# Layer 3 of a four-layer graph network: groups 2 to 4 copied from PSUM as they are, one root for them, weighting one step behind counting, and a loop ordered by an account

## The chip, the cores and the metric

The kernel runs on one NeuronCore of one Trainium2 chip. The core has a matrix engine (PE), a vector engine (DVE), a scalar engine (ACT), a general engine (POOL) and a queue engine (SP) that starts most of the transfers. Each engine takes its instructions in the order in which they were written, and waits at an instruction until what it needs is there. The metric is device time in microseconds (us), the median of several runs of the whole kernel.

## The reference, cut to what matters

A node matrix `x` of 3327 x 64 floats goes through four layers over one adjacency matrix `adj` of 3327 x 3327 floats. Each layer ends in `x = layernorm(x + layer(x))`. Layers 0 and 1 work on distances, layer 2 is two rounds of `tanh([adj @ x, x] @ W)`. The change lies in layer 3 and in the way into it:

```python
x = _layernorm(x + _L2_gnn_ref(x, adj, L2_gnn_W), axis=-1)
# layer 3
support = x @ weight
mask = (adj != 0)
rank = cumsum(mask, axis=1)          # neighbours counted along a row
deg = rank[:, -1:]
k = minimum(deg, 100)
pos = rank - (deg - k)
w = mask * where(pos > 0, 0.5 ** (k - pos), 0.0)
x = _layernorm(x + w @ support + bias, axis=-1)
```

So a neighbour's weight is one half to the power of the number of neighbours that come after it in the row. For every entry of the mask the kernel must know how many neighbours follow.

## The kernel before, in words

**Tiling.** The 3327 nodes are padded to 26 blocks of 128. The adjacency lies transposed in memory, so a block `jb` is 128 source nodes (on the partitions) by 3328 target nodes. Targets are cut into two halves of 1664, and a half into four chunks of 416. Layer 3 runs over 52 steps `q`: 26 blocks for half 0, then 26 for half 1 (`steps`, a list of `(h, jb)`). The passage between the halves is called the turn.

**One step of layer 3.** A step needs the mask of its half block: 1.0 where the adjacency is not zero, as bf16 (`masks`, L366, on DVE). Nine of the 26 blocks have their masks left over from layer 2 (`resident`); the other 17 are loaded again, half by half, as `ah` (L345, on SP's queue, four load buffers, `LOADS`), which makes 34 loads and 34 masks in the layer. Row 0 of a mask is overwritten by a small transfer from `t_rows` (L368), which holds how many neighbours the later blocks have; it is on SP's queue also, and behind it, in the same call, the next load is issued. `count` (L650) multiplies the mask by a constant triangle `tri` on PE: the result in PSUM is, entry by entry, the exponent bits of the weight. `read` brings it to SBUF as int16, whose bits are read as bf16 weights `w` (L669 on ACT, a Relu; or L667 on DVE, a max with 0). A step has two halves `c` of two chunks `e`, so it has four counts and four reads. The counts have one pair of PSUM banks for each `c`: `count(c, q+1)` can only begin when both reads of `(c, q)` are done. `products` then multiplies the weights by the support rows. Those are kept as a sum of three bf16 parts: `s12` holds the first two side by side (the high product, L875, two a half step), `s3` the third (the low product, L892, 64 columns wide). Low products are saved up for `GROUP` steps and then run together.

**The order of the work.** All engines' orders in this part are written out by hand, and a step of the loop (L1051) writes reads, a mask if a buffer is free (`MASKS` buffers), one or two left-over pieces, and then on PE `products(q - LEAD, c)` and `advance(c, q)`, which is `count(c, q + 1)`, for `c` 0 and 1. `LEAD` is 3: products are three steps behind the reads. Whether the second read of a half step goes to DVE or ACT is decided by a small running load of each engine (`loads`).

**The way in.** The tanh of layer 2 comes out in four chunks (`chunk_end`, L629), and `with_x2` (L729) adds the residual. `finish` (L736) multiplies 13 column pairs by `both_m`, which gives centred hidden values and support rows before their norm; this is done in four groups A, B, C, E of 3, 3, 3 and 4 pairs, into two PSUM buffers of two banks each. For each group, `squares` (L745) and `sums` (L748) give the variance, `roots` (L753 to L771) one over its root in nine small DVE instructions, `factor` (L776) the support rows in `rr`, and `x3_of` or `hid_out` and `x3_later` (L776, L791) the layer's input `x3`. `first_part`, `rest_of` and `other_parts` (L794, L798, L802, L803) cut `rr` into its three parts. C and E have one root together. The PSUM of the two `finish` buffers is used again by the accumulators `acc` of the products.

**Row 0.** Row 0 of every block is treated apart: `first_masks` loads these rows, `first_weights` (L477 to L481) makes their weights in `tb`, `first_rows` (L906, L909) gathers their support rows by 16 transfers on POOL's queue, and `first_products` (L916) adds them when four steps of a half are left.

**The end of a half.** `sums_out` (L928 on ACT, L929 on DVE) adds the bias, `by_node` (L935) turns and centres the result, and the norm and the stores follow: `half_out` for half 0 in between the steps of half 1, `last_out` at the very end.

Of the kernel before, what the change touches and what calls it, by code (L numbers as in the profile page):

```python
# [40 lines left out]
LATE = 3  # L41
UNDER_WAY = 4
MORE = 1
CLAMP = 127.0
FIRST_T = 8
BATCH_T = 2
MASKS = 6
LOADS = 4

LN_EPS = 1e-5  # L50
# [18 lines left out]
CUBIC_PLUS = 2 * CUBIC_ROOT - 1  # L69
CUBIC_REST = 1.75705840270866  # L70
NEIGH = 100
GROUP = 7
LEAD = 3
AHEAD = 5
STEP = float(2**7)

# [5 lines left out]
def kernel(  # L82
# [230 lines left out]
    def layers(ctx, x2, x3, begun_here, kept, ready, ahead_ctx, strm):  # L313
# [160 lines left out]
            return m0  # L474

        def first_weights(m0):
            nc.vector.tensor_scalar(m0, m0, 0.0, (NEIGH + 1) * STEP, ALU.not_equal, ALU.mult)  # L477
            yield
            nc.vector.scalar_tensor_tensor(m0, tb, -STEP, m0, op0=ALU.mult, op1=ALU.add)
            yield  # L480
            nc.vector.tensor_scalar(tb.bitcast(I16), m0, 0.0, None, ALU.max)  # L481
            yield

        with tc.tile_pool(
# [200 lines left out]
        rest = [jb for jb in range(NB) if jb not in resident]  # L685
        rest.sort(key=lambda jb: next(i for i, g in enumerate((10, 7, 4, 0)) if jb % NBH >= g))
        for h in range(2):
            n = len(here) - (5 if h == 0 else 0)
            mixed = here[:-n]
            late_here = here[-n:]  # L690
            for i, jb in enumerate(rest):
                mixed.append(jb)
                while late_here and (i + 1) * n >= (n - len(late_here) + 1) * len(rest):
                    mixed.append(late_here.pop(0))
            steps += [(h, jb) for jb in mixed]
        for q, (h, jb) in enumerate(steps):
# [23 lines left out]
        def slots(i):  # L720
            g, n = parts[i]
            return slice(2 * g, 2 * (g + n))
# [21 lines left out]
        def squares(i):  # L744
            nc.scalar.activation(halves(sq[:, slots(i)]), both[i][0], AF.Square, scale=0.125)  # L745

        def sums(i):
            nc.vector.tensor_reduce(var[:, slots(i)], sq[:, slots(i)], axis=AX.X, op=ALU.add)  # L748

        def roots(sl):  # L750

            v = var[:, sl]
            nc.vector.tensor_scalar(v, v, LN_EPS, None, ALU.add)  # L753
            for _ in roots_of(v, sl):
                pass

        def roots_of(v, sl):

# [14 lines left out]
        def scaled(i, src, dst):  # L773
            n = parts[i][1]
            r = halves(y_all[:, slots(i)].unsqueeze(2).to_broadcast([P, 2 * n, D]))
            nc.vector.scalar_tensor_tensor(  # L776
                halves(dst[:, slots(i)]), src, ROOT_FACTOR, r, op0=ALU.mult, op1=ALU.mult
            )

        def factor(i):  # L780

            scaled(i, both[i][1], rr)

        def x3_of(i):
            scaled(i, both[i][0], x3)

        def x3_later(i):
            scaled(i, halves(x3[:, slots(i)]), x3)

        def hid_out(i):  # L790
            nc.scalar.copy(halves(x3[:, slots(i)]), both[i][0])  # L791

        def first_part(i):
            nc.scalar.copy(s12[:, slots(i), 0, :], rr[:, slots(i)])  # L794

        def rest_of(i):
            sl = slots(i)
            nc.vector.tensor_tensor(rr[:, sl], rr[:, sl], s12[:, sl, 0, :], ALU.subtract)  # L798

        def other_parts(i):  # L800
            sl = slots(i)
            nc.scalar.copy(s12[:, sl, 1, :], rr[:, sl])  # L802
            nc.gpsimd.tensor_tensor(s3[:, sl], rr[:, sl], s12[:, sl, 1, :], ALU.subtract)  # L803

        with tc.tile_pool(name="l3t", bufs=2, space=PSUM, reuse_waits="tile") as l3t:
            chunk_end(3)
            with_x2(3)
            chunk_end(2)
            with_x2(2)
            masks(to_mask.pop(0))  # L810
            finish(l3t, A)
            squares(A)
            chunk_end(1)
            sums(A)
            roots(slots(A))
            factor(A)
            with_x2(1)
            finish(l3t, B)
            squares(B)
            x3_of(A)  # L820
            sums(B)
            first_part(A)
            count(0, 0)
            read(0, 0, (False, False))
            rest_of(A)
            chunk_end(0)
            roots(slots(B))
            with_x2(0)
            other_parts(A)
            finish(l3t, C)  # L830
            count(1, 0)
            squares(C)
            factor(B)
            x3_of(B)
            read(1, 0, (False, False))
            sums(C)
            first_part(B)
            finish(l3t, E)
            rest_of(B)
            hid_out(C)  # L840
            squares(E)
            advance(0, 0)
            masks(to_mask.pop(0))
            masks(to_mask.pop(0))
            sums(E)
            read(0, 1, (False, False))
            advance(1, 0)
            roots(slice(0, 2 * sum(parts[C])))
            read(1, 1, (False, False))
            advance(0, 1)  # L850
            read(0, 2, (False, False))
            advance(1, 1)
            read(1, 2, (False, False))
            factor(C)
            factor(E)
            hid_out(E)
            advance(0, 2)

        l3a = ctx.enter_context(
            tc.tile_pool(name="l3a", bufs=2, space=PSUM, reuse_waits="tile")  # L860
# [5 lines left out]

        def products(q, c):
            h, jb = steps[q]
            first, last = q % NB == 0, q % NB == NB - 1
            if first:  # L870
                acc[h, c] = acc_tile(f"acc3_{h}_{c}")[:, :, :CW]
# [12 lines left out]
            later.append((q, c))  # L884
            if not last:
                high(q, c)
            if last or c and len(later) == 2 * GROUP:
                for ql, cl in later:
                    if last and cl != c:
                        continue  # L890
                    for e in range(2):
                        nc.tensor.matmul(  # L892
                            acc[h, cl][e * D : (e + 1) * D, e, :], s3[:, slot(steps[ql][1]), :],
                            ws[ql, cl, e], start=False, stop=False,
                        )
                later[:] = [ql for ql in later if last and ql[1] > c]
                if last:
                    high(q, c)
# [88 lines left out]
        def last_out(h, accT):  # L987
# [45 lines left out]

        first_out = None
        weighted = first_weights(m0)
        with_step = [
            (lambda: other_parts(B), 0.0, 0.5), (lambda: first_part(C), 0.0, 0.5),
            (lambda: rest_of(C), 0.6, 0.0), (lambda: other_parts(C), 0.0, 0.5),
            (lambda: first_part(E), 0.0, 0.6), (lambda: rest_of(E), 0.7, 0.0),
            (lambda: other_parts(E), 0.0, 0.6),  # L1040
        ]
        at_leisure = [
            (lambda: next(weighted), 0.6, 12), (lambda: next(weighted), 1.05, 14),
            (lambda: next(weighted), 0.6, 16), (lambda: x3_later(C), 0.6, NB),
            (lambda: x3_later(E), 0.7, NB + 1),
        ]
        loads = {True: 0.0, False: 0.0}
        products(0, 0)
        advance(1, 2)
        products(0, 1)  # L1050
        for q in range(LEAD, len(steps) + LEAD + 1):  # L1051
            turn = q == NB + LEAD
            while consumed and consumed[0] <= q:
                consumed.pop(0)
            at_work = len(consumed) - len(to_mask) + (len(at_leisure) > 2)
            one_more = bool(to_mask) and at_work < MASKS
            extra, d, a = with_step.pop(0) if with_step else (None, 0.0, 0.0)
            if NB + LEAD <= q < NB + LEAD + 9:
                d, a = d + 0.6, a + 0.2
            loads[True] = max(0.0, loads[True] - 1.8) + d + 1.04 * one_more  # L1060
            loads[False] = max(0.0, loads[False] - 1.8) + 1.04 + a
            reads = []
            for _ in range(2):
                by = loads[True] + 0.6 <= loads[False] + 0.8
                loads[by] += 0.6 if by else 0.52
                reads.append(by)
            read(0, q, (False, reads[0]))
            if turn:
                first_out = half_out(0, sums_out(0))
            read(1, q, (False, reads[1]))  # L1070
            if extra is not None:
                extra()
            if one_more:
                masks(to_mask.pop(0))
            if not with_step and at_leisure:
                late, d, by = at_leisure[0]
                if loads[True] + d < 2.0 or q >= by:
                    at_leisure.pop(0)
                    late()
                    loads[True] += d  # L1080
                    if len(at_leisure) == 2:
                        first_rows()
            p = q - LEAD if q < NB + LEAD else q - LEAD - 1
            for c in range(2):
                if p and not turn:
                    products(p, c)
                if q < len(steps):
                    advance(c, q)
                if turn:
                    next(first_out)  # L1090
            if first_out is not None and not turn:
                next(first_out, None)
        last_out(1, sums_out(1))


# [991 lines left out]
```

## Time and profile before

| what | us |
|---|---|
| time before, median of 3 runs | 542.13 |
| lowest and highest of them | 540.40, 545.91 |
| the profiled execution's own time | 545.59 |
| its span (first to last instruction of the profile) | 543.9 |
| mean granted PE clock in it | 0.979 |
| first layer 3 instruction on PE (`finish` of group A, L736) | 402.85 |
| first count (L650) | 407.99 |
| first high product (L875) | 419.63 |
| last high product ends | 529.91 |

Times in the profile are counted from the start of its span. A profile group reads: line, engine, operation, output<-input, shape, count, busy time, mean duration of one in ns, idle time of the engine just ahead of it and what ended that. A chain is followed back from the last instruction to what released each. A window table gives the busy time of each engine in a stretch, the count of instructions, the granted PE clock and the transfer engines' share.

### The profile page before, as it was taken

Reading aid. Unit: us, or ns where it says so; the run is one execution under the profiler, and the core shown is the slowest. Engines: PE = TensorE matmul, PEld = TensorE weight load, DVE = VectorE, ACT = ScalarE, POOL = GpSimd, SP = SyncE. Lnnn points to the kernel's source line nnn. Section 1 sums busy time; section 2 is a strip of 40 time slices with the busy share of each in tenths; the row PEclk is TensorE's granted clock in tenths of the full one; section 3 lists DMA queues with packets and bytes.
Section 4 is the critical chain, followed back from the end, with each engine's and each line's share of the span. In section 5 each row is a group of like instructions: output and inputs, shape, how many; then the busy total and the mean of one; then the engine's idle time right before and its main releaser. Section 6 shows DMA issues by size and latency. Waiting matters only on the chain.

```text
span 543.9 us, 7678 instructions
## 1 busy us (share of the span) xinstructions
PE 506.3 (93%) x2865; PEld 210.9 (39%) x2865; DVE 398.8 (73%) x604; ACT 294.2 (54%) x410; POOL 230.5 (42%) x121
## 2 busy tenths in 40 slices
PE   7989999999999999989999999999998898998991
PEld 5622222222222222754433344333343444454551
DVE  6889999999999999899453413456249876577633
ACT  5799999999999998540000010000017766376632
POOL 4499999999999999100000000000360350000000
PEclk9899999999999999999999999999999999799996
DMA  8979777676767718499999207988967899777001
GB/s 286 351 232 295 222 234 230 217 238 203 248 209 234 244 36 331 183 430 420 424 429 425 93 1 282 427 352 330 380 211 254 298 359 339 278 250 225 1 1 38
DMA packets 34139, 139.21 MB, mean 256 GB/s; under 512 B 11199, under 2 KB 12977, under 8 KB 28971
## 3 DMA queue, kind: packets, MB, share of 16 engines
q1 hardware_dynamic: 30571, 137.40, 69.3%
q0 software_dynamic: 1184, 0.63, 0.5%
q10 hardware_dynamic: 2336, 0.59, 0.5%
q8 instruction: 24, 0.39, 0.3%
q14 instruction: 24, 0.20, 0.1%
HBM read 136.93 MB, written 1.04 MB: 254 GB/s over the span
## 4 chain that ended last, share of the span: by engine, by line
PE 60%; DVE 18%; ACT 10%; issue 6%; DMA 4%; DVEq 0%; SPq 0%; ACTq 0%
PE cnt L516 27%; DVE v L1336 10%; PE pq L1315 7%; PE acc L875 5%; PE cnt L650 4%; ACT pq L1328 4%; ACT sg L1288 4%; PE acc L892 4%; PE acc L1345 3%; DMA ah<-in_adjT 3%; PE t L450 2%; DVE a L1327 2%; DVE mask L366 2%; PE cnt L507 1%; DVE w L667 1%
## 5 line engine op out<-in xcount | busy, mean ns | idle before, releaser
L1300 POOL TENSOR_TENSOR sg<-sg,at 128x1664 f32<-128x1664 f32 x44 | 163.7, 3736 | 1.7 <-ACT sg L1288 1.6
L1328 ACT ACTIVATE pq<-pq,al,ga 128x832 f32<-128x832 f32 x104 | 104.7, 1012 | 11.0 <-DVE a L1327 11.0
L1315 PE MATMUL pq<-riT,ljT 64*128 64x416 f32 x416 | 100.8, 561 | 10.3 <-DVE v L1336 6.2
L1336 DVE SCALAR_TENSOR_TENSOR v<-pq,a 128x832 f32<-128x832 f32 x104 | 105.5, 1014 | 3.5 <-ACT pq L1328 2.5
L1327 DVE SCALAR_TENSOR_TENSOR a<-pq,sg 128x832 f32<-128x832 f32 x104 | 105.2, 1012 | 0.5 <-PE prep_fours L1406 0.5
L1345 PE MATMUL acc<-v,xv 128*64 128x416 f32 x416 | 95.3, 537 | 0.0
L516 PE MATMUL cnt<-at_l,lj 128*64 128x416 f32 x496 | 90.5, 515 | 0.0
L669 ACT ACTIVATE w<-cnt 128x416 int16<-128x416 f32 x145 | 66.9, 523 | 38.1 <-PE cnt L650 35.5
L1288 ACT ACTIVATE sg<-lb,rb 128x1664 f32<-128x1664 f32 (+1 forms) x53 | 87.2, 1647 | 0.0
L629 ACT ACTIVATE x<-cnt 128x416 f32<-128x416 f32 x8 | 4.1, 517 | 142.9 <-PE cnt L516 142.9
L462 POOL DMA_DIRECT2D t_rows<-tb x4 | 4.2, 1089 | 150.0 <-DVE tb L460 150.0
L1315 PEld LDWEIGHTS pq<-riT,ljT 64*128 64x128 f32 x416 | 31.3, 184 | 83.7 <-DVE v L1336 82.8
L875 PE MATMUL acc<-w,s 128*128 128x416 bf16 x208 | 53.0, 341 | 1.6 <-DVE sq L776 0.8
L516 PEld LDWEIGHTS cnt<-at_l,lj 128*64 128x64 f32 x496 | 34.4, 137 | 49.8 <-issue 49.4
L667 DVE TENSOR_SCALAR w<-cnt 128x416 int16<-128x416 f32 x63 | 36.4, 585 | 15.4 <-PE cnt L650 14.3
L1345 PEld LDWEIGHTS acc<-v,xv 128*64 128x64 f32 x416 | 20.6, 134 | 61.8 <-issue 58.0
L366 DVE TENSOR_SCALAR mask<-ah 128x1664 bf16<-128x1664 f32 x34 | 35.2, 1040 | 11.7 <-PE cnt L650 6.0
L650 PE MATMUL cnt<-mask,tri 128*128 128x416 bf16 x136 | 36.4, 340 | 6.8 <-DVE w L667 6.5
L516 PE MATMUL cnt<-kept,lj 128*64 128x416 f32 x224 | 41.6, 514 | 0.0
L443 DVE TENSOR_SCALAR tm<-at_l 128x1664 bf16<-128x1664 f32 x16 | 15.7, 1023 | 21.6 <-PE t L450 21.5
L875 PEld LDWEIGHTS <-s 128*128 128x128 bf16 x208 | 19.8, 98 | 29.5 <-issue 14.6
L1300 POOL TENSOR_TENSOR sg<-sg,kept 128x1664 f32<-128x1664 f32 (+1 forms) x10 | 30.0, 3018 | 0.0
(314 smaller groups left out, 457.5 us busy)
## 6 DMA issues: line engine op xcount, KB each, us to landing
at_l<-in_adjT SPq DMA_DIRECT2D x27, 1664.0 KB, 11.8
at<-in_adjT SPq DMA_DIRECT2D x44, 832.0 KB, 6.6
ah<-in_adjT SPq DMA_DIRECT2D x34, 832.0 KB, 7.3
kept<-in_adjT SPq DMA_DIRECT2D x7, 1664.0 KB
bt_l<-in_adjT SPq DMA_DIRECT2D x6, 1664.0 KB
lb<-lf_rows SPq DMA_DIRECT2D x2, 384.0 KB, 6.1
mask<-t_rows SPq DMA_DIRECT2D x34, 3.2 KB
ljT<-ljT SPq DMA_DIRECT2D x4, 128.0 KB, 3.8
```

Source lines behind the costliest of these rows:

```text
L366: nc.vector.tensor_scalar(mask[q], ahead.pop(q), 0.0, None, ALU.not_equal)
L516: nc.tensor.matmul(acc[c][h * D : (h + 1) * D, :], hw[:, slot(jb), :], blocks[jb][:, o : o + CW], start=c not in begun, stop=last, skip_gr ...
L650: nc.tensor.matmul(cnt[c][e], tri, mask[q][:, of], start=True, stop=True, skip_group_check=True,)
L669: nc.scalar.activation(to, of, AF.Relu)
L875: nc.tensor.matmul(acc[h, c][:, e, :], s12[:, slot(jb)].rearrange("p t d -> p (t d)"), ws[q, c, e], start=first, stop=last,)
L1288: nc.scalar.activation(sg[:, :, of], lbs[:, :, of], AF.Sigmoid, bias=rb[:, sl : sl + 1])
L1300: nc.gpsimd.tensor_tensor(sg[:, :, of], sg[:, :, of], at[:, :, of], ALU.mult)
L1315: nc.tensor.matmul(pq[:, h, :], ljT[h != jb // NBH][rows, of], riT[rows, ch * CW : (ch + 1) * CW], start=True, stop=True,)
L1327: stt(a_s[t], pqs[t], CUBIC_PLUS, us.pop(t), op0=ALU.add, op1=ALU.mult)
L1328: nc.scalar.activation(pqs[t], pqs[t], AF.Square, bias=al[:, one], scale=ga[:, one])
L1336: stt(w, pqs.pop(t), CUBIC_REST, a_s.pop(t), op0=ALU.add, op1=ALU.mult)
L1345: nc.tensor.matmul(accs[cp, ci][h * D : (h + 1) * D, :], xv[:, slot(jb), :], w[:, h, :], start=(jb == orders[cp][0]), stop=(jb == orders[c ...
```

## The change

Several edits in layer 3 alone; all work ahead of it is untouched.

1. `finish` of groups B, C and E: both results are copied from PSUM to SBUF as they are by ACT (`parts_out`: x3 and `rr`), two copies each. Squares and sums of B and C together (12 slots), then of E, read the copies; one root covers all 20 slots (`roots(BCE)`), and the factors are applied in SBUF later (`scaled_of`).
2. The cut into three parts: the second part is the DVE subtraction itself, written as bf16; POOL does two subtractions instead of one; the ACT cast is gone.
3. `LEAD` goes from 3 to 1, `GROUP` from 7 to 4, so there are 7 weight buffers instead of 12 of each kind, and `MASKS` goes from 6 to 11.
4. The order of the steps: half 0 begins with the six blocks of group A, the resident ones first.
5. The loop keeps an account of when DVE and ACT will be free (`end`), when a count is there (`counted`), when a load is expected (`landed`), and when PE is free (`at_pe`), and from it chooses at each half step whether DVE first takes a left-over piece, a mask, or the read.
6. After the turn the products of `c` = 1 are one more step behind those of `c` = 0.
7. `CLAMP` is 101 instead of 127, and the weights of row 0 are made in two instructions instead of three.

```diff
-MASKS = 6
+MASKS = 11
-GROUP = 7
-LEAD = 3
+GROUP = 4
+LEAD = 1
...
+        def parts_out(i):
+            nc.scalar.copy(halves(x3[:, slots(i)]), both[i][0])
+            nc.scalar.copy(halves(rr[:, slots(i)]), both[i][1])
...
+        def other_parts(sl):
+            one, two = s12[:, sl, 0, :], s12[:, sl, 1, :]
+            nc.vector.tensor_tensor(two, rr[:, sl], one, ALU.subtract)
+            nc.gpsimd.tensor_tensor(rr[:, sl], rr[:, sl], one, ALU.subtract)
+            nc.gpsimd.tensor_tensor(s3[:, sl], rr[:, sl], two, ALU.subtract)
...
             finish(l3t, B)
-            squares(B)
-            x3_of(A)
-            sums(B)
-            first_part(A)
+            first_part(slots(A))
+            parts_out(B)
             count(0, 0)
-            read(0, 0, (False, False))
-            rest_of(A)
+            read(0, 0, (False, True))
+            other_parts(slots(A))
+            masks(to_mask.pop(0))
             chunk_end(0)
-            roots(slots(B))
             with_x2(0)
-            other_parts(A)
             finish(l3t, C)
             count(1, 0)
-            squares(C)
-            factor(B)
-            x3_of(B)
-            read(1, 0, (False, False))
-            sums(C)
-            first_part(B)
+            masks(to_mask.pop(0))
+            parts_out(C)
+            read(1, 0, (False, True))
+            advance(0, 0)
             finish(l3t, E)
-            rest_of(B)
-            hid_out(C)
-            squares(E)
-            advance(0, 0)
-            masks(to_mask.pop(0))
-            masks(to_mask.pop(0))
-            sums(E)
-            read(0, 1, (False, False))
+            squares_of(BC)
+            parts_out(E)
             advance(1, 0)
...
+        def fill(q, ready):
+            while True:
+                if extras and extras[0][1] == DVE:
+                    cost, by = extras[0][2:]
+                    if max(end[DVE], one_done) + cost <= ready + 0.2 or q >= by:
+                        extra()
+                        continue
+                soon = to_mask and to_mask[0] - q
+                if mask_ready(q) and (
+                    max(end[DVE], landed[0]) + MASK <= ready + 0.5
+                    or soon < 3
+                ):
+                    one_mask()
+                    continue
+                return
...
+            for c in range(2):
+                was_read = reads(c, q) if q < len(steps) else 0.0
...
+                if not turn and p[c] >= (NB if q > NB + LEAD else 0) and p[c] < len(steps):
+                    products(p[c], c)
...
+                if q + 1 < len(steps):
+                    advance(c, q)
```

## The prediction

> **What bounds the kernel now.** I read the page first (busy shares, chain, groups), then the chain of waits and the window table inside layer 3 (402.85 us to the end), then the timeline around each hole. PE is busy 93% of the span, so I asked where in layer 3 it is not. The windows, 3 us each (busy time, number of instructions, PE clock, transfer share, GB/s):
>
> ```profile
> core 0: us, PE busy (x) PEld busy (x) DVE busy (x) ACT busy (x) POOL busy (x), PEclk, DMA share, GB/s
> ...
> 417.00:420.00 3.00, 1.94 (x8) 0.60 (x7) 2.59 (x12) 2.30 (x6) 0.00 (x0) 1.00 0.94 329
> ...
> 429.00:432.00 3.00, 2.05 (x10) 0.87 (x9) 2.21 (x4) 2.87 (x8) 0.04 (x1) 1.00 0.90 307
> ...
> 459.00:462.00 3.00, 1.44 (x8) 0.68 (x7) 0.12 (x1) 1.36 (x4) 0.00 (x0) 1.00 1.00 412
> 462.00:465.00 3.00, 1.54 (x7) 0.50 (x8) 2.50 (x4) 0.00 (x0) 0.00 (x0) 0.61 1.01 409
> 465.00:468.00 3.00, 3.00 (x20) 1.53 (x18) 0.43 (x1) 0.00 (x0) 0.00 (x0) 0.50 0.92 346
> ```
>
> At 459 to 465 every engine is idle and transfers run full; then PE works at half clock. The timeline there shows the hole's two ends:
>
> ```profile
> 461.88 1.03 DVE L366 TENSOR_SCALAR mask<-ah 128x1664 bf16<-128x1664 f32 x1 [3.06 <-DMA ah<-in_adjT]
> 462.82 0.58 DVE L667 TENSOR_SCALAR w<-cnt 128x416 int16<-128x416 f32 x1
> ...
> 463.46 0.51 PE L650 MATMUL cnt<-mask,tri 128*128 128x416 bf16 x1 [3.02 <-DVE w L667]
> ```
>
> A mask stood in DVE's order ahead of a read, and its load had not landed; the read was late by that, and PE's count by the read. The chain has the same figure at 424.21 (a transfer of 6.50 us, then mask, read, count). The way in is a chain of DVE work:
>
> ```profile
> 416.44 0.60 DVE l_var L748
> ...
> 418.74 0.18 DVE root_y L771
> ...
> 419.01 1.16 DVE sq L776 x2
> ```
>
> The first high product (419.63) waits for group C's factor at the end of this root, as the accumulator takes that group's PSUM. From 498 on PE has no hole: the high products of a step follow at 1.41 us and a run of 28 low ones takes 2.58 us. So layer 3 is PE-bound in its last 30 us, and before that held up by DVE.
>
> **What the Trainium skill says.** *TensorE: Matmul & The Clock Gate*, "HAM oscillation — how this bites in real kernels": no PE-idle gaps over about 3.4 us, or the clock is halved and time is lost again. The trace agrees, even a little below that: a 3.02 us hole with thin work around it is followed by 6.8 us at clock 0.50 (462.7 to 469.5), a loss of 3.4 us. *DMA: Bandwidth & Descriptors*, "Queues, rings and completion order": a transfer engine takes descriptors in ring order. The trace agrees: a `t_rows` packet lands 1.0 us after its issue on an empty queue and up to 5 us with loads ahead of it. *VectorE: DVE Perf Modes*, "Why PSUM operands drop a tier": fp32 from PSUM gets one element a cycle, a one-tensor SBUF operation two; here a 416 read takes 0.583 us, a 1664 mask 1.03.
>
> **The change part by part.** Prices from the rows of before: read 0.523 on ACT (0.46 each in a run), 0.585 on DVE; mask 1.04; 384-wide pieces 0.50 to 0.55, 512-wide 0.60 to 0.68; a root nine times 0.2 = 1.8.
>
> *Work.* DVE: before, four sums 2.3, three roots 5.4, factors 2.3, x3 2.3, differences 2.3, weights of row 0 2.2: 16.8 us. After, sums 2.2, two roots 3.6, factors 2.2, x3 2.2, differences 2.2, weights 1.6: 14.0. Saved 2.8. ACT: before 7.6 (squares 2.07, copies 1.09, two casts a group 4.4), after 7.1 (squares 1.9, six copies 3.2, one cast 2.0): even. The wide forms (768, 896) are not in the trace; between the 512 row (0.62, 0.68) and twice 384 (1.0, 1.1) for 768, I take 0.82 on ACT and 0.95 on DVE; 0.1 either way. POOL doubles from 4.1 to some 8.3; the last group's pair (2.2 each, scaled from 0.98 for 384) follows the cast in step 6 or so and is needed by the low products of step 11, five steps later: hidden by about 4 us. If DVE's masks held POOL for the 9 us that one L803 waited, the cover would be gone and some 4 us lost.
>
> *Start.* I walked the new order with these prices. Unchanged to 408.0. ACT: cast A to 408.6, copies B 409.6, first read 410.1, last tanh 411.3; PE ends C at 412.24; copies C 413.2, read, squares of B and C to 414.4; PE ends E near 414.8, copies E to 416.0. PE: counts of step 1 by 415.3, first high product 415.2 to 415.6 (C's PSUM free since 413.2; the second needs E's, 416.0). So it comes 4.3 us sooner, with counts done for two steps instead of three and a half (6 matmuls, 1.1 us). Net some 3 us.
>
> *Floor.* From 415.2 PE has 200 counts and 208 high at 0.176 (71.8), 208 low at 0.0923 (19.2), a change of form around each of some 13 low runs at 0.11 (1.4), first products 1.3, `by_node` at the turn 2.8: 96.5, so 511.7. The same sum for before, from 419.63: 514.5. Its real end is 529.91, so its holes are worth 15.4. They are, by the starts of the high products: steps 0 to 6 2.3, at 431 1.4, 444 1.5, 455 to 460 0.9, 460 to 470 6.1 (3.4 of it clock), turn 2.7, 491 1.6.
>
> *New waits.* DVE's `other_parts(B)` waits for ACT's cast, which stands behind the four reads of step 4 (ACT near 423.3, DVE free at 422.75: 0.6 idle); behind it in DVE's order are the last factor, a mask (step 8's) and the read of step 6, for which PE waits; that is in (a). Copies C and E on ACT stand ahead of the first reads of steps 0 and 1, in the walk above.
>
> *What stays of the holes.* (a) Steps 0 to 8: walking on, reads of steps 4 and 5 are all on ACT (4 x 0.46 to 0.52 = 2.0 against PE's 1.41), with squares and two casts (2.2) between; I get 432.0 where the floor says 429.8: 2.2. (b) Steps 8 to 11 again all on ACT: 1.1. (c) Steps 12 to 25: DVE's order holds 7.3, 6.4 and 7.0 us of work in each four steps, where PE takes 4 x 1.41 + 1.5 = 7.1: full, but not over; 2.0 for queueing. (d) The turn: `c` = 1's products a step later take the 1.1 wait for the norm's sums off PE; 0.7 stays. (e) Half 1: DVE 7.9 and 7.5 in its first eight steps, thinner later; 1.1. Sum 7.1.
>
> *The masks.* Loads: 34 at about 2.2 us when the queue is full; median 7.3 to landing with four under way, about 3.8 on an empty queue. Half 0 needs 12 masks in steps 10 to 24, 3 in four steps of 7.1 us: 2.4 us each, against 2.2. The fifth load lands at 415 and its mask is in DVE's order near 425; load 9 follows that and lands near 430, for step 14 at about 441. Eleven buffers let this lead stand; six did not. So the load holes (at 424 and 460) should go. In SP's order nothing new stands before a load; stores of half 0 are two there as before. Masks put on DVE before a load lands cost DVE up to 0.8 (the account takes 3.55 from mask to landing; the trace has 4.3); in (c).
>
> *The low groups.* Four instead of seven steps cost 6 more changes of form (0.66, in the floor) and spread the relief for reads better. `LEAD` 1 costs nothing: a count already waits for the reads of the step before, so the weights are there. Row 0's chain ends near 450, its products come at about 460; cover 10 us.
>
> *Sum.* 511.7 + 7.1 = 518.8; what follows the last product (543.9 - 529.9 = 14.0) is the same code: span 532.8, and 1.7 outside it: 534.5, to be set against the profiled 545.59. That execution is 3.5 above the median 542.13. If the difference is the half-clock stretch (3.4), which need not fall in each run, the new kernel owes nothing for it: 534.5; if it is spread over the kernel, 531. I take **533.5**.
>
> **The rivals.** *Forecast (0.70):* 528 to 537.
>
> *ACT and DVE take PE's place (0.15).* For it: both have over 7 us in some four-step groups; the account's prices are guesses, and DVE's order is fixed. Against: half 1 of before runs clean with ACT doing 3 of 4 reads. Twice my holes, 14: 541; 537 to 543.
>
> *Late masks in DVE's order (0.07), the slower one.* The new order has three masks in a row in step 12 and pairs in step 16, 20, 24, 32. If loads come later than accounted, each is a 3.0 us hole and 3.4 of half clock, 6.4 in all. Two such beyond my 7.1 give 547.3; it decides from the second on, three give 553.7. Against: masks lead by up to 11 steps' buffers, and before had one such double loss with six.
>
> *It begins sooner, but nothing else (0.03).* Start 2.8, holes as before: 542.8 in the profile's terms, 539 to 542.
>
> *Better (0.05).* Holes 2 or less, and a run like the median: 526.
>
> **Numbers.** A measurement here can tell about 1% from no change, which is 536.7 to 547.5. Faster: nearly all of the forecast, the better case and a little of the second: 0.82. Same 0.10, slower 0.08. Range: holes of 1 with the median's offset, 527, to holes of 13, 540.5.
>
> **What would show it.** First high product near 415 instead of 419.6; no DVE wait for `ah` above 1.5 us, no half clock between 410 and 520; high products at 1.41 us within groups in both halves; 16 low ones in 1.5; ACT full between 416 and 435; last high product at 517 to 521. It is wrong if a DVE mask still waits for its load, or if reads on DVE are the releaser of PE at every group.

## The result, and the profile after

The changed kernel takes 544.28 us (median of 15 runs, 542.81 to 546.08) beside 542.95 for the kernel before on the same chip (15 runs): ratio 1.0025, 95% interval 1.0009 to 1.0041. So it is not faster, and the 1.3 us by which it is slower are below the 1% that the forecast took as the bound. The forecast was 533.5; none of the ranges that the prediction gave to its cases holds the measured time. The profiled execution took 545.25 us with a span of 543.5; the sum in the prediction gave 534.5 and 532.8 for these two, so 10.7 us of span are to be found.

Four times cut the layer, read off the starts of the counts and of the high products in the trace. The forecast's row is the prediction's own walk (408.0, 415.2, floor and holes 103.6, then 14.0). The prediction counted to the end of the last high product, 0.34 us after its start; the other rows are from start to start, so the forecast's two last numbers are put here as 103.3 and 14.3:

| us | first count at | from it to the first high product | steps 0 to 25 | 25 to 27, the turn | 27 to the last | first to last high product | from there to the end |
|---|---|---|---|---|---|---|---|
| before | 407.99 | 11.64 | 57.95 | 8.08 | 43.92 | 109.94 | 14.29 |
| forecast | 408.0 | 7.2 | | | | 103.3 | 14.3 |
| after | 407.67 | 13.12 | 55.61 | 9.45 | 43.86 | 108.93 | 13.81 |

The start is 5.9 us longer than forecast, and the products 5.7 us longer, most of it before step 25 and some at the turn. What came after the turn took as long as it did before the change. Two faults are looked for in what follows: one ahead of the first high product, and one between 430 and 445.

The start first. The window table of the changed kernel (columns: stretch, busy time with count of PE, PE loads, DVE, ACT, POOL, then PE clock, transfer share, GB/s):

```profile
core 0: us, PE busy (x) PEld busy (x) DVE busy (x) ACT busy (x) POOL busy (x), PEclk, DMA share, GB/s
400.00:405.00 5.00, 5.00 (x28) 2.39 (x26) 2.40 (x4) 1.52 (x3) 3.17 (x5) 1.00 0.15 41
405.00:410.00 5.00, 5.00 (x28) 2.31 (x24) 4.23 (x15) 2.28 (x5) 0.72 (x2) 1.00 0.13 37
410.00:415.00 5.00, 2.62 (x14) 1.45 (x10) 0.26 (x2) 2.52 (x5) 1.82 (x2) 0.98 0.70 249
415.00:420.00 5.00, 3.45 (x8) 2.67 (x9) 3.43 (x5) 0.00 (x0) 0.00 (x0) 0.50 1.02 427
...
440.00:445.00 5.00, 3.33 (x10) 1.27 (x11) 4.80 (x7) 1.44 (x3) 5.00 (x9) 0.71 0.82 247
```

From 400 to 410 the transfers are idle (0.15 and 0.13; the kernel before has 0.92 and 1.03 there), from 410 to 415 DVE is idle (0.26 us of 5), and then PE runs at half clock. The timeline of the changed kernel, SP's queue and then DVE, says why DVE was idle:

```profile
395.66 16.09 SPq L345 DMA_DIRECT2D ah<-in_adjT  x4
...
409.59 0.55 DVE L808 TENSOR_TENSOR s<-sq,s 128x384 bf16<-128x384 f32 x1
414.88 1.03 DVE L366 TENSOR_SCALAR mask<-ah 128x1664 bf16<-128x1664 f32 x1 [4.74 <-DMA ah<-in_adjT]
415.82 0.58 DVE L733 TENSOR_TENSOR x<-x,xc 128x416 f32<-128x416 f32 x1
```

DVE's second mask waits 4.74 us for its load, and `with_x2` (here L733) of the last chunk stands behind it. `finish` of group E (here L740) waits for that, and the first high product (here L868) comes after it, as PE's timeline shows:

```profile
416.55 3.75 PE L740 MATMUL both<-both_m,x 128*128 128x256 f32 x8 [3.93 <-DVE x L733]
420.09 0.90 PE L649 MATMUL cnt<-kept,tri 128*128 128x416 bf16 x2
420.79 0.90 PE L868 MATMUL acc<-w,s 128*128 128x416 bf16 x2
```

The four first loads took 16.09 us to be issued. In the kernel before:

```profile
398.77 1.99 SPq L345 DMA_DIRECT2D ah<-in_adjT  x4
```

SP's own waits in the changed kernel, 390 to 420 (who waited for what: us in total, times, longest), name the reason:

```profile
engine line waited for: us in total, times, longest us
SPq L345 <- PE cnt L515: 18.1, 2, 14.5
```

A load waits 14.5 us for a count of layer 2 (`cnt`, L515), with which it shares no data. It shares memory. In the built program the four `ah` buffers lie at bytes 159904 to 186528 of a partition before and at 176544 to 203168 after: five more mask buffers lie below them. In their new place three of them, those of the second, the third and (by 448 bytes) the fourth load, overlap two blocks kept for layer 2 (189408 to 202720 and 202720 to 216032), which its last products read until 410.4. SP issues in order, so the held load holds those behind it.

The second place, 433 to 442, in the timeline of the changed kernel:

```profile
434.06 2.60 POOL L809 TENSOR_TENSOR sq<-sq,s 128x896 f32<-128x896 f32 x1 [1.82 <-DVE s L808]
434.84 2.05 DVE L478 TENSOR_SCALAR tb<-tb 128x832 int16<-128x832 bf16 x1
...
436.74 1.90 POOL L810 TENSOR_TENSOR s<-sq,s 128x896 bf16<-128x896 f32 x1
436.82 2.70 DVE L366 TENSOR_SCALAR mask<-ah 128x1664 bf16<-128x1664 f32 x1
...
441.10 0.34 PE L649 MATMUL cnt<-mask,tri 128*128 128x416 bf16 x1 [2.18 <-DMA mask<-t_rows]
```

The first weighting of row 0 (L478), for which the loop's account has 0.6, took 2.05, and the mask behind it 2.70 where a mask takes 1.03. Both lie beside POOL's two wide subtractions. PE then waits 2.18 us for row 0 of a late mask (the small transfer from `t_rows`), and the mean clock from 440 to 445 is 0.71.

### The profile page after: what moved, and what is told of

It is laid out like the page before. It is cut to its first block, busy times and chain, and to the rows that moved or that the text cites. A ratio compares the mean times of both kernels' runs of the same rounds, so it can differ in the third digit from the quotient of the medians.

```text
span 543.5 us, 7648 instructions
## 1 busy us (share of the span) xinstructions
PE 506.7 (93%) x2865; PEld 210.7 (39%) x2865; DVE 404.9 (74%) x598; ACT 292.2 (54%) x400; POOL 236.0 (43%) x123
## 5 line engine op out<-in xcount | busy, mean ns | idle before, releaser
L515 PE MATMUL cnt<-at_l,lj 128*64 128x416 f32 x496 | 90.5, 515 | 0.0
L668 ACT ACTIVATE w<-cnt 128x416 int16<-128x416 f32 x137 | 64.7, 520 | 32.5 <-PE cnt L649 31.0
L868 PE MATMUL acc<-w,s 128*128 128x416 bf16 x208 | 54.4, 346 | 0.0
L515 PEld LDWEIGHTS cnt<-at_l,lj 128*64 128x64 f32 x496 | 34.4, 137 | 49.8 <-issue 49.4
L666 DVE TENSOR_SCALAR w<-cnt 128x416 int16<-128x416 f32 x71 | 41.2, 588 | 13.3 <-PE cnt L649 10.5
L366 DVE TENSOR_SCALAR mask<-ah 128x1664 bf16<-128x1664 f32 x34 | 36.7, 1092 | 9.5 <-DMA ah<-in_adjT 9.5
L515 PE MATMUL cnt<-kept,lj 128*64 128x416 f32 x224 | 41.6, 515 | 0.0
L649 PEld LDWEIGHTS <-tri 128*128 128x128 bf16 x208 | 19.5, 99 | 24.3 <-issue 7.0
```

The costliest lines, as they stand in the source:

```text
L366: nc.vector.tensor_scalar(mask[q], ahead.pop(q), 0.0, None, ALU.not_equal)
L515: nc.tensor.matmul(acc[c][h * D : (h + 1) * D, :], hw[:, slot(jb), :], blocks[jb][:, o : o + CW], start=c not in begun, stop=last, skip_gr ...
L649: nc.tensor.matmul(cnt[c][e], tri, mask[q][:, of], start=True, stop=True, skip_group_check=True,)
L668: nc.scalar.activation(to, of, AF.Relu)
L868: nc.tensor.matmul(acc[h, c][:, e, :], s12[:, slot(jb)].rearrange("p t d -> p (t d)"), ws[q, c, e], start=first, stop=last,)
```

## The experiments

Each ran beside the kernel before on the same chip. Since that one's median moved by 1.2 us between calls, the ratio is the better measure across them. e9 and e11 have four timed runs each and e14 six, the others 9 to 20; hence the wide intervals of these three.

| run | median us | ratio to before, 95% interval |
|---|---|---|
| the changed kernel | 544.28 | 1.0025, 1.0009 to 1.0041 |
| e1 MASKS = 6 | 540.29 | 0.9963, 0.9945 to 0.9981 |
| e2 C, E on DVE | 545.10 | 1.0048, 1.0029 to 1.0067 |
| e3 e1 and e2 | 540.45 | 0.9976, 0.9959 to 0.9993 |
| e4 before, loads late | 545.38 | 1.0050, 1.0025 to 1.0075 |
| e5 e1, row 0 late | 539.93 | 0.9942, 0.9916 to 0.9968 |
| e6 e1, six load buffers | 541.89 | 0.9995, 0.9969 to 1.0020 |
| e7 e1, square later at the turn | 542.77 | 0.9998, 0.9980 to 1.0017 |
| e8 e1, GROUP = 7 | 549.02 | 1.0104, 1.0073 to 1.0135 |
| e9 e1, C, E on DVE, row 0 late | 535.84 | 0.9861, 0.9800 to 0.9923 |
| e10 e1, six buffers elsewhere | 538.51 | 0.9909, 0.9880 to 0.9939 |
| e11 e9 and e10 | 534.45 | 0.9829, 0.9775 to 0.9883 |
| e12 e9 without row 0 late | 540.77 | 0.9956, 0.9938 to 0.9974 |
| e13 e9 with MASKS = 11 | 541.65 | 0.9972, 0.9945 to 0.9999 |
| e14 e11 again | 535.17 | 0.9854, 0.9821 to 0.9887 |

### The late loads: e1, e4

The written order of the changed kernel never has more than six masks alive, so `MASKS` 6 leaves every engine's order as it is and only moves the buffers.

```diff
-MASKS = 11
+MASKS = 6
```

> The changed kernel with MASKS 6 instead of 11, nothing else. The instruction order is the same on every engine; what moves is where the tiles lie: the four load buffers return to the addresses that they had in the kernel before, off the tiles that layer 2's last products still read. Theory L (late loads: loads 2 to 4 of layer 3 were issued at 410.5 instead of 399 us because of the address): they are issued near 399 again, no hole at 413 to 417, the first high product near 415.2, and the loads stay ahead, so the waits for ah near 451 and 454 go too: 533 to 537 us. Rival D (DVE and its order are the bound, the loads only hide it): the holes move but the time stays within 1% of 544.

540.29, 4.0 us less (3.4 by the ratios). The four loads go out at once again, and from the first count to the first high product it takes 8.40 us, not 13.12. But the time lies above L's 533 to 537, and within 1% of 544 as D had it: the address is one loss, and not the only one. In e1's timeline:

```profile
400.05 2.11 SPq L345 DMA_DIRECT2D ah<-in_adjT  x4
```

The reverse, on the kernel before: the `ah` buffers in a pool of their own, at 179872 to 206496, with every engine's order as it was.

```diff
-                ahead[q] = l3w.tile([P, HALF], F32, tag="ah", ...)
+                ahead[q] = l3h.tile([P, HALF], F32, tag="ah", ...)
...
-                w = l3w.tile(
+                w = (l3v if c else l3w).tile(
```

> The kernel before with its load buffers placed across the same still used tiles as in the changed kernel (the weight buffers of c = 0 lie below them instead), the instruction order unchanged. Theory L: loads 2 to 4 are issued near 410.5, every later load is some 8 us behind, and the time goes up by 4 to 9 us, to 547 to 552. Rival D: the loads have slack, under 2 us.

545.38, 2.9 above its own reference. e4's timeline shows the row of the changed kernel again:

```profile
397.25 16.09 SPq L345 DMA_DIRECT2D ah<-in_adjT  x4
```

The place of the buffers alone makes both the loss and its return. It is less than the 547 to 552 expected: from first count to first high product it took 13.40 us for 11.64, only 1.8 more. In the old way in `with_x2` (412.89 in e4) stands ahead of the late masks; they wait 0.56 and 1.01 us for their loads at 416.40 and 418.44, ahead of the last root.

### POOL beside DVE: e2, e3, e5, e9, e12, e13

The two subtractions of groups C and E go from POOL to DVE, in the changed kernel (e2) and with six masks (e3).

```diff
-            nc.gpsimd.tensor_tensor(rr[:, sl], rr[:, sl], one, ALU.subtract)
-            nc.gpsimd.tensor_tensor(s3[:, sl], rr[:, sl], two, ALU.subtract)
+            eng = nc.vector if sl == CE else nc.gpsimd
+            eng.tensor_tensor(rr[:, sl], rr[:, sl], one, ALU.subtract)
+            eng.tensor_tensor(s3[:, sl], rr[:, sl], two, ALU.subtract)
```

> The changed kernel with the two POOL subtractions of groups C and E (896 wide, other_parts) on DVE instead, the loads still late. Theory P (POOL's wide subtractions hold DVE: a mask took 2.70 and the row 0 weights 2.05 us beside them, instead of 1.03 and 0.6): DVE gets 2.2 us of work and loses 3.1 us of stretching, the PE hole of 438 to 441 and the half clock behind it shrink: 538 to 542. Rival (the 2.05 is the price of that form, and the hole is the mask's late row): no gain, 544 to 547.

> MASKS 6 and the subtractions of C and E on DVE together. Theories L and P together: 530 to 534. L alone right: as e1 or up to 2 us slower.

There is no gain in either: e2's time is its rival's, and e3's is that of L alone. But the durations are settled by it, and against e2's rival: 2.05 us is not the price of that form. The same two DVE instructions, first in e1 with POOL beside them, then in e3 without:

```profile
431.17 2.60 POOL L809 TENSOR_TENSOR sq<-sq,s 128x896 f32<-128x896 f32 x1 [1.82 <-DVE s L808]
431.94 2.06 DVE L478 TENSOR_SCALAR tb<-tb 128x832 int16<-128x832 bf16 x1
433.84 1.90 POOL L810 TENSOR_TENSOR s<-sq,s 128x896 bf16<-128x896 f32 x1
433.92 2.71 DVE L366 TENSOR_SCALAR mask<-ah 128x1664 bf16<-128x1664 f32 x1
```

```profile
431.95 0.37 DVE L478 TENSOR_SCALAR tb<-tb 128x832 int16<-128x832 bf16 x1
432.24 1.02 DVE L366 TENSOR_SCALAR mask<-ah 128x1664 bf16<-128x1664 f32 x1
```

0.37 for 2.06, and 1.02 for 2.71. In e1 the weighting ends at 434.00, 0.23 after POOL's first subtraction, and the mask at 436.63, 0.89 after the second: each is held until POOL is nearly done. The Trainium skill has this on *SBUF — State Buffer*, "Who interferes with whom": DVE in a 2-port mode and GpSimd share a pair of ports, and whichever issues first has it for the whole instruction while "the other fully blocks". The trace agrees: POOL's ends plus the two lengths alone give 434.14 and 436.76, 0.14 and 0.13 from what is seen. So the two subtractions cost DVE 1.69 + 1.69 = 3.4 us here, and spare it two of 1.09 us. (A mask beside the 384-wide pair of group B, 1.74 us at 426.83, loses 0.7 us more, in e3 as in e1.)

That this difference of 1.2 us bought nothing in e3 asks what else stands in that stretch. Row 0's two instructions are not due before step 22, so e5 moves them (and the two scalings of x3 behind them in the list) to step 17 and later.

```diff
-            (lambda: next(weighted), DVE, 0.6, 13), (lambda: next(weighted), DVE, 1.05, 15),
+            (lambda: next(weighted), DVE, 0.6, 18), (lambda: next(weighted), DVE, 1.05, 19),
...
-                if extras and extras[0][1] == DVE:
+                if extras and extras[0][1] == DVE and (q >= 17 or len(extras) not in (3, 4)):
```

> The kernel with MASKS = 6, and the two instructions that weight row 0 (with the two x3 scalings that stand behind them in the list) moved from steps 9 to 13 to steps 17 and later; all work is kept. Theory D: with the loads early again, VectorE sets the counts from 430 to 447: its 0.59-us weighting took 2.06 and the mask behind it 2.71, both beside GpSimd's subtractions, and the counts of steps 10 to 12 wait for the mask behind them. The four steps from 9 to 13 took 12.0 us, of which 5.64 are products and counts and 1.63 a group of low products, so 4.7 are lost there. Moved away, most of that should come back: 536.0 to 538.0 (3 to 4.5 us under the 540.29 of MASKS = 6). Rival Q: the masks only meet the next wait (the load behind each of them, or the row of the mask that is fetched from memory after it): 539 to 540.5.

539.93, a miss for D. e5's timeline shows why:

```profile
431.06 7.20 DVE L366 TENSOR_SCALAR mask<-ah 128x1664 bf16<-128x1664 f32 x4
431.22 2.60 POOL L809 TENSOR_TENSOR sq<-sq,s 128x896 f32<-128x896 f32 x1 [1.82 <-DVE s L808]
...
433.90 2.54 POOL L810 TENSOR_TENSOR s<-sq,s 128x896 bf16<-128x896 f32 x1
...
438.81 0.51 PE L649 MATMUL cnt<-mask,tri 128*128 128x416 bf16 x1 [3.13 <-DVE w L666]
```

Masks moved into the place, four in 7.20 us, where three in a row take 2.89 without POOL (e9, below); one in turn held POOL (2.54 us for 1.90), and a read behind them let PE wait 3.13 us. So e9 does both, and counts the subtractions in the order's account as DVE work:

```diff
-            (lambda: other_parts(CE), DVE, 1.05, 11),
+            (lambda: other_parts(CE), DVE, 3.2, 11),
```

> MASKS = 6, the two subtractions of the group pair C, E on VectorE in place of GpSimd and counted at 3.2 us by the list of the order, and row 0 weighted from step 17 on. No GpSimd subtraction stands beside a mask of this stretch any more. Theory G (GpSimd's subtractions stretch VectorE's masks from 1.02 to 2.71 us and so set the counts of steps 8 to 12): with row 0 moved alone the four masks from 431.1 took 7.20 us instead of 4.1 and a count waited 3.13 us behind them, so that nothing was gained; with both moved, the 3.13-us wait and the half clock behind it (0.85 and 0.81 over ten us, 1.7 us) go, and VectorE's own 2.2 us of subtractions lie between masks with some slack: 535.5 to 537.5, against 539.93 with row 0 alone moved. Rival Q (behind every such wait stands another, the loads and the rows of the masks): 539 to 541, no mask above 1.1 us all the same.

535.84, as G said, though from four runs (534.84 to 538.65). Half clock and the long hole are gone. In e9's timeline three masks in a row take 2.89 us, and in its windows the clock stays at 1.00 though PE idles 1.9 us of five:

```profile
431.34 2.89 DVE L366 TENSOR_SCALAR mask<-ah 128x1664 bf16<-128x1664 f32 x3
```

```profile
435.00:440.00 5.00, 3.14 (x18) 1.39 (x17) 3.84 (x5) 3.18 (x8) 0.56 (x1) 1.00 0.94 344
440.00:445.00 5.00, 5.00 (x37) 2.61 (x36) 4.87 (x7) 3.23 (x8) 3.56 (x5) 1.00 1.00 378
```

e12 keeps the account's new price but leaves row 0 where it was (e9 without its two lines of e5).

> MASKS = 6 and the subtractions of C, E on VectorE, counted at 3.2 us by the list of the order, row 0 weighted as soon as it fits (as in the changed kernel). Tells which part of the 4.1 us between 539.93 and 535.84 (row 0 late alone, and both) is GpSimd's. If the masks of steps 8 to 12 beside GpSimd were the whole loss: 535.5 to 536.5. If row 0's place matters beside it: 537 to 539.

540.77: above both cases. By the medians neither half of e9 is worth anything alone (e5 0.4, e12 none), both are worth 4.4. A part of this is the clock, which falls or stays up behind much the same hole: e5's four runs with a mean granted clock of 0.983 to 0.987 took 537.1 to 538.1 us, its eight at 0.980 and below 539.7 to 540.8. The lowest times (e1 538.39, e5 537.08, e12 538.40, e9 534.84) give 1.3 us to e5, nothing to e12 and 3.55 to both. So both together are worth more than their sum, but e5 alone is not worthless. e9 without the account's new price was not run. In e12 no mask from 427 on takes over 1.03 us, and it keeps pace with e9 to step 10 (high product 29.76 and 29.77 us after the first count). But then row 0 and an x3 scaling (0.37 + 1.02 + 0.95 = 2.3 us) stand ahead of the next mask, and the other scaling (0.68) ahead of the one behind it. They come late, so their buffers are emptied late and the loads for later masks are issued late. (Half clock from 437.1 to 440.6, which e9 does not have, adds at most 1.7 us to e12's loss of 5.9 before step 25.) DVE's waits for loads in e12, 407 to 480, against 1.7 us in e9:

```profile
DVE mask L366 <- DMA ah<-in_adjT: 6.1, 5, 1.7
```

These runs fit one reading, which no single run proves: what runs out is DVE's time up to the last mask whose load is pressing, whatever fills it, POOL's block, row 0, or its own subtractions.

e13 is e9's order on all engines with the buffers of the changed kernel (`MASKS` 11).

> The changed kernel with its eleven mask buffers, so with the loads late at the start, and with C, E on VectorE and row 0 late. If the late loads (4.0 us by MASKS = 6 alone) and VectorE's stretch (4.4 us from 540.29 to 535.84) add: 539 to 540.5. If the late loads hide the second, since VectorE then waits for loads anyway: 542 to 544.

541.65: between the two cases. By the ratios the late loads cost 1.1% in e9 (0.9861 to 0.9972, 6.0 us) and 0.6% in the changed kernel (3.4 us). So the two losses do not hide one another. By the medians the two remedies are worth 4.0 and 2.6 us alone and 8.4 together; that each helps the other is a sign only, since the difference (0.5%) is within the interval of e9's ratio (0.6% either way).

### Load buffers: e6, e10, e11, e14

In e1 the transfer share falls to 0.07 from 425 to 430 and is 0.9 to 1.0 after 440: a load is issued only when a mask has emptied a buffer. e6 gives six buffers.

```diff
-LOADS = 4
+LOADS = 6
...
-            chunk_end(0)
+            chunk_end(0); load(); load()
```

> The kernel with MASKS = 6 and six load buffers in place of four, the two further loads issued behind layer 2's last products. Theory B: in the run with MASKS = 6 the DMA share fell to 0.07 from 425 to 430, since a load is only issued when a mask has emptied a buffer, and was 0.9 to 1.02 from 440 on; with two loads more under way the masks from 440 to 455 find their loads landed, and the counts that waited 0.65 and 0.52 us behind them at 449 and 451 with them: 1 to 1.5 us less than 540.29. Theory D (VectorE is late by its own work, not by loads): within 0.6 of 540.29.

541.89, slower than e1, by a mistake of mine that confirms the first cause. The two new buffers, at 186528 to 199840, fall to the second and third load and lie over a block that layer 2 still reads. e6's timeline shows the issue of the first four loads, and its waits of SP name the same count:

```profile
399.67 13.30 SPq L345 DMA_DIRECT2D ah<-in_adjT  x4
```

```profile
SPq L345 <- PE cnt L515: 14.4, 2, 11.7
```

From first count to first high product it took 12.49 us again. e10 uses the two buffers only for loads issued after layer 2's last products.

```diff
-                ahead[q] = l3w.tile([P, HALF], F32, tag="ah", bufs=LOADS, ...)
+                n = len(loaded); loaded.append(q); far = n > 4 and (n - 4) % 6 in (2, 3)
+                ahead[q] = l3w.tile([P, HALF], F32, tag="ax" if far else "ah", bufs=2 if far else LOADS, ...)
...
-            masks(to_mask.pop(0))
+            masks(to_mask.pop(0)); load(); load()
```

> MASKS = 6 and two load buffers more, as in the earlier run with six, but placed so that only loads issued after layer 2's last products use them, and no load waits for a tile that layer 2 still reads. Theory L: the earlier run lost its gain since the fifth load went into a buffer over tiles that layer 2's last products still read, and held the queue: first count to first high product 12.49 us against 8.40. Here it is 8.4 again, and the masks from 440 to 455 don't wait for loads: 539.0 to 539.8 against 540.29. Rival: loads are late by the transfers' rate (DMA share 0.9 to 1.0 from 440 on), so buffers don't matter: within 0.5 of 540.29, with the same waits for loads after 445.

> The two before it together. If G holds and loads are the next wait: 534.5 to 536.5, at least 1 us under the run without the six buffers. If neither: 539 to 541.

> The kernel of all three edits again, for a closer time: 533.5 to 535.5.

e10 took 538.51, under both of its cases; e11 534.45, at the lower end of its first case; e14 535.17, in its range. In e10 no mask from 440 to 455 waits for its load, in e1 three do (0.81, 0.56 and 1.02 us). In the traces steps 0 to 25 take 1.2 to 1.3 us less with six buffers (53.38 against 54.65 in e1; 49.04 and 49.10 against 50.28 in e9); by the timed runs e9 and e14 are not told apart. e11 and e14 are the fastest here (one kernel, twice), 1.2 to 2.25% and 1.1 to 1.8% under the kernel before.

### The turn and the low groups: e7, e8

```diff
-            elif first_out is not None and next(first_out, 0) is None:
+            elif first_out is not None and q > NB + LEAD + 1 and next(first_out, 0) is None:
```

> The kernel with MASKS = 6, and at the turn between the halves the addition and the square of the first half's output one step later, so that ScalarE doesn't stand in its square for the 26 products of the output (3.7 us) with the weighting of step 27 behind it. Theory T: the hole of 1.4 us at 479.9 to 481.3 goes: 539.0 to 539.6, against 540.29. Rival: the 26 products themselves (3.0 us in one piece with no other work under way) are all of the turn's loss, and what is moved by a step makes a wait there: 540 to 541.

542.77. The turn took 9.55 us instead of 9.45: the hole only moved. In e7's timeline:

```profile
483.03 0.53 PE L868 MATMUL acc<-w,s 128*128 128x416 bf16 x2 [1.12 <-DVE hid L963]
```

That its time lies 2.5 us above e1's is not explained by this: 1.3 us were lost before step 25, where the order is the same, and 1.4 after step 27. The first is about what the clock makes: behind the same hole of 2.15 us it was at half for 6.8 us in e7 and for 3.4 in e1. The second stays open.

```diff
-GROUP = 4
+GROUP = 7
```

> The kernel with MASKS = 6 and GROUP = 7 in place of 4: low products of seven steps at a time, 8 groups in place of 13 or 14. By the price of a group (16 low products took 1.63 us, 28 took 2.69 in the kernel before, against 0.0923 us for each product alone) 13 groups pay 2.0 us beside their products and 8 groups 0.85: 539.0 to 539.4 if TensorE is the bound throughout. Rival: the groups lie in holes where TensorE would wait for masks anyway, so the time stays within 0.5 of 540.29; or, a longer group lets VectorE and ScalarE get ahead: 538 to 539.

549.02, far outside both. The account puts masks in the longer low runs, several in a row, where they meet loads that have not landed, and the reads stand behind them. e8's timeline, DVE and then PE:

```profile
467.52 1.03 DVE L366 TENSOR_SCALAR mask<-ah 128x1664 bf16<-128x1664 f32 x1 [2.61 <-DMA ah<-in_adjT]
469.59 1.03 DVE L366 TENSOR_SCALAR mask<-ah 128x1664 bf16<-128x1664 f32 x1 [1.04 <-DMA ah<-in_adjT]
...
471.17 0.34 PE L649 MATMUL cnt<-mask,tri 128*128 128x416 bf16 x1 [2.52 <-DVE w L666]
```

This is the prediction's slower rival, in a kernel that I had not meant it for. It tells nothing of the low products' own price.

## Why the prediction was wrong

The cuts of the earlier table, for the kernels that carry the argument:

| us | first count at | to first high product | steps 0 to 25 | turn | 27 to last | first to last | to the end | span |
|---|---|---|---|---|---|---|---|---|
| forecast | 408.0 | 7.2 | | | | 103.3 | 14.3 | 532.8 |
| after | 407.67 | 13.12 | 55.61 | 9.45 | 43.86 | 108.93 | 13.81 | 543.5 |
| e1 | 409.27 | 8.40 | 54.65 | 9.45 | 43.97 | 108.08 | 13.91 | 539.7 |
| e13 | 407.70 | 13.20 | 52.07 | 9.45 | 44.02 | 105.54 | 13.83 | 540.3 |
| e9 | 408.91 | 8.40 | 50.28 | 9.45 | 44.07 | 103.81 | 13.90 | 535.0 |
| e11 | 407.69 | 8.40 | 49.04 | 9.45 | 43.83 | 102.32 | 13.82 | 532.2 |

The 10.7 us of span are some 5.9 at the start, 4.5 in steps 0 to 25 and 1.6 at the turn, less 0.8 in half 1, 0.5 at the end and 0.3 ahead of the first count; 0.3 are left to the rounding of the prices.

*Start: the step that failed.* "Unchanged to 408.0", and under *The masks* "In SP's order nothing new stands before a load". Nothing new stands there, but the buffer had moved onto a tile still being read, which is a wait that neither the diff nor the order of SP shows. The first high product came at 420.79 instead of 415.2. With the buffers moved back the walk is 1.2 us short (8.40 for 7.2), which is only a size. The mask put ahead of `with_x2` turned a late load into a late way in; for masks written ahead of their loads the prediction had set at most 0.8 us on DVE, and the one wait was 4.74. "Eleven buffers let this lead stand; six did not" was wrong as well: the order never uses more than six.

*Work: the second failure.* POOL's doubled work was called "hidden by about 4 us", and I asked only whether DVE's masks hold POOL. What cost time was the other way round: POOL held DVE. Row 0's weights were priced 1.6 and took 2.05 + 1.01, of which the first is 0.37 without POOL. DVE's busy time rose by 6.1 us (398.8 to 404.9), but most of that is no failure of this step: DVE made 71 reads where it made 63 before (41.7 us for 36.9), which the forecast of 2.8 less left out. Without reads and masks DVE's work in the layer fell by 1.1 us (29.9 to 28.8, by sums of durations, as the other sums here), and it would have fallen by 2.8 without POOL's 1.7 on row 0; the masks took 1.8 us more (37.1 for 35.4).

*Holes (a) to (c).* 5.3 us were put on steps 0 to 25. By the prediction's own prices their work (100 counts and 100 high products, 100 low ones in seven runs, row 0's products 0.65) is 45.9 us; after shows 9.8 us of holes and half clock, e9 4.4, e11 3.2. The size I had was about that of the kernel without the two faults; "full, but not over" for DVE in steps 12 to 25 was true only then.

*The low groups.* A group of 16 took 1.62 where the floor has 16 x 0.0923 + 0.11 = 1.59 (and the signs 1.5), and there were 15 runs of low products, not 13: size only, some 0.9 us in all. *The turn*: 0.7 us of holes was left for it, and 9.45 us against 8.08 before went there. In PE's timeline two waits stand in it, 0.56 us for a read on DVE and 0.86 for one on ACT, where before has one of 0.48; two counts more fall into the cut. Which part of the change brings the waits stays open, since e7 only moved one of them. *Half 1* shows no large hole (43.86 us from step 27 on, 43.92 before), and the end, 13.81, was put at 14.3. One sum in the prediction is wrong: its list of the holes before adds up to 16.5, not 15.4; only the case that begins sooner and gains nothing else rests on it.

*The rivals.* Two of them came in part. A late mask in DVE's order did cost a hole and half clock, but at 412, not from step 12, and through an address. DVE did take PE's place, from 430 to 445 (14.8 us busy of 15). Together they ate the gain of the rest, which by e11 was real: its span is 532.2 where the sum said 532.8. That agreement is partly luck, as six load buffers were not in the sum; e9 has 535.0.

*What would show it.* Right: high products at 1.41 us within groups. Wrong: the first high product (420.79), ACT full from 416 (it was idle from 415 to 420), DVE's wait for `ah` (4.74), half clock (0.50 at 415 to 420, 0.71 at 440 to 445), the last high product (529.71; in e9 521.1, in e11 518.4).

## What to carry to other kernels

When a change alters the number or size of buffers, list the addresses before and after, and who still reads what lies there: a transfer into a reused place is issued only when the last reader is done, and an in-order queue holds everything behind it. When work goes to GpSimd, price what it does to VectorE's one-input SBUF instructions next to it, in both directions. Where one engine's order carries both urgent reads and the refilling of load buffers, removing a microsecond from it may show little until the next item in the same stretch is removed too, so try remedies together as well as singly.

## What the runs showed of the hardware

A VectorE instruction of 0.37 us took 2.06 us beside a GpSimd subtraction, and a mask 2.71 for 1.02 (e3 and e1); VectorE's reads from PSUM kept their length beside one (three in a row took 1.59 us in e1, the first two of them while GpSimd ran, and 1.60 in e9 at 499.1 without it). TensorE's clock fell to half behind a hole of only 2.15 us (e1, from 439.3 to 442.8) and behind two of 1.16 and 0.67 close together (e12), but it stayed at 1.00 behind one of 2.17 (e10) and behind two of 1.19 and 0.67 (e9). So holes well under the 3.0 us of the kernel before can cost the clock, and in these runs their length alone does not decide whether they do.
